# A graph layer with decayed neighbour weights: weight multiplied in at the start, variance by a product with ones, bias with the accumulator's copy, groups closed by transposes, and a new order of all tasks

## The chip, the cores and the metric

The kernel runs on one core of one Trainium2 chip. The metric is device time in microseconds; a timed run is about 2 us longer than the span between the first and the last instruction in its trace. Moments are us from the start of the span.

## The reference, cut to what matters

```python
def _L0_gnn_ref(input, adj, weight, bias):        # MAX_NEIGH 100, DECAY 0.5
    support = input @ weight                      # 4096 x 64 @ 64 x 64
    mask = (adj != 0).astype(support.dtype)       # 4096 x 4096
    rank = jnp.cumsum(mask, axis=1)
    deg = rank[:, -1:]
    k = jnp.minimum(deg, float(MAX_NEIGH))
    pos = rank - (deg - k)
    w = mask * jnp.where(pos > 0, DECAY ** (k - pos), 0.0)
    return w @ support + bias
h = jnp.maximum(_layernorm(x, axis=-1), 0.0)
x = x + _L0_gnn_ref(h, adj, L0_gnn_weight, L0_gnn_bias)
```

The adjacency is 67 MB of float32; x is 1 MB. Everything else is small.

## The kernel before

The adjacency streams in as 64 chunks of 1 MB (128 rows by 2048 columns); four chunks make a unit, two units make a group of 512 output rows. A chunk is converted to bytes by VectorE, some by ScalarE (`signed`), transposed as packed words by TensorE, and settled into SBUF by VectorE. A unit's counts go through `totals` (TensorE), `split` (ScalarE), `suffix` (TensorE) and `clamp` (VectorE). Then, eight times a unit, `place` and `scan` (TensorE) give the exponent, `weigh` (ScalarE) the weight 2^-n, and `aggregate` (TensorE) adds weights times features into one PSUM bank. At a group's end `drain`, `project` (times the weight matrix) and `finish` follow.

The features are prepared once, at the start: turned, centered, squared, reduced, put to the power -1/2 on GpSimd, scaled, and cut in a rounded half and a remainder.

```python
    def center(b0):
        pc = pxs[b0] = ps_v.tile([P, 4, H, D], F32, tag="v", name="pc")
        for b in range(4):
            nc.tensor.matmul(pc[:, b, :, :], xt[:, (b0 + b) * P:(b0 + b + 1) * P], less, start=True, stop=True)
    # ... centered: ScalarE copies pc to xs; square: ScalarE
    def root(h):
        ...
        nc.vector.reduce_sum(var, sqs.pop(h), axis=AX.X)
        nc.vector.tensor_scalar(var, var, EPS, 2.0 ** -76, op0=ALU.add, op1=ALU.mult)
        nc.gpsimd.tensor_tensor(ns[h], var, half.to_broadcast([P, HB]), op=ALU.pow)
    # ... scale, first (rounded copy, ScalarE), second (difference, VectorE)
    def project(g, part=None):
        ...
            nc.tensor.matmul(pts[g][:, tt, :], sums[g][:, tt * P:(tt + 1) * P], w_sb, start=True, stop=True)
```

No engine's instruction order is written by hand. Each task has an engine, a rank, two modelled durations and its needs; a loop in the kernel's own Python picks, engine by engine, the task of lowest rank among those ready within a short wait, and the program is emitted in that order. Each engine then executes its list in order, so a rank or a modelled duration changes the order, and the order is fixed once built.

```python
        task(totals, (u,), PE, 8 * u - 7, 750, 950, ...)
        for k in range(NP):
            task(scan, (u, k), PE, 8 * u + k, 240, 450, [("place", u, k // CB)])
            task(weigh, (u, k), ACT, 8 * u + k, 1000, 1130, [("scan", u, k)], ("w", ("aggregate", u, k)))
            task(aggregate, (u, k), PE, 8 * u + k + 3, 475, 710, ...)
```

## Time and profile before

| | before |
|---|---|
| timed, median of 3 | 210.91 us (210.53 to 211.01) |
| span of the profiled run | 208.8 us |
| TensorE, ScalarE, VectorE busy | 89%, 81%, 71% |
| stream of chunks | 420 GB/s until about 168 us |
| first weigh of unit 0, 1, 15 | 29.0, 46.2, 193.9 us |

Shares of busy time do not decide here, since three engines and the stream run at nearly the same pace. What is read instead is the lag: how long after the landing of a unit's fourth chunk its first weigh starts. The landing is the last of the sixteen that the trace has for each load.

### The profile page before, as it was taken

What the parts mean: (1) busy time and instruction counts of PE and PEld (TensorE: products, weight loads), DVE (VectorE), ACT (ScalarE), POOL (GpSimd) and SP (SyncE); (2) the same over time, 40 slices, a digit from 0 to 9 for tenths busy, and PEclk for the clock granted to TensorE, in tenths of its full rate; (3) what the DMA queues carried; (4) which work ended last, traced back from release to release, by engine and by line L of the source; (5) the groups of instructions that cost most, each with busy time, mean ns of one, the idle gap of its engine ahead of it and who ended that gap; (6) DMA issues with size and microseconds to landing.
All of it is one profiled execution on the core that took longest, in us unless ns stands there. A gap on an engine that the chain in (4) does not pass through costs nothing.

```text
span 208.8 us, 2970 instructions
## 1 busy us (share of the span) xinstructions
PE 186.9 (89%) x1101; PEld 106.9 (51%) x1101; DVE 149.2 (71%) x192; ACT 169.6 (81%) x172; POOL 23.8 (11%) x39
## 2 busy tenths in 40 slices
PE   7299784987999999979999989999999999999972
PEld 2189441544556464645465546556555655554321
DVE  4943999998888797888887896989698974411001
ACT  2066959996997989879999897898989898998870
POOL 6000075050005000200040002000200020001000
PEclk9969999999999999999999999999999999999996
DMA  6999999899999999999999999999999910000000
GB/s 237 424 425 424 419 417 424 342 418 421 425 422 425 419 421 421 424 421 419 422 422 422 421 421 422 424 416 424 417 422 419 383 69 3 0 0 25 0 0 25
DMA packets 10445, 69.45 MB, mean 333 GB/s; under 512 B 1504, under 2 KB 1760, under 8 KB 2240
## 3 DMA queue, kind: packets, MB, share of 16 engines
q1 hardware_dynamic: 9952, 68.29, 78.8%
q0 software_dynamic: 336, 0.92, 1.1%
q8 instruction: 8, 0.13, 0.2%
q10 hardware_dynamic: 144, 0.07, 0.1%
q14 instruction: 5, 0.04, 0.0%
HBM read 68.22 MB, written 1.05 MB: 332 GB/s over the span
## 4 chain that ended last, share of the span: by engine, by line
DMA 52%; PE 30%; DVE 9%; ACT 3%; issue 3%; POOL 1%; DVEq 0%; SPq 0%; ACTq 0%; POOLq 0%
DMA a_sb<-in_adj_dram 52%; PE acc L352 11%; DVE m L288 5%; PE v L339 4%; PE pt L298 4%; ACT wk L344 3%; PE px L233 2%; PE po L375 2%; PE v L336 2%; PE pc L243 2%; PE tot L313 1%; PE ps L324 1%; DVE mt L307 1%; DVE o L381 1%; PE none L225 1%
## 5 line engine op out<-in xcount | busy, mean ns | idle before, releaser
L344 ACT ACTIVATE wk<-v,floor 128x1024 fp32r<-128x1024 uint8 x128 | 134.0, 1120 | 19.3 <-PE v L339 19.1
L352 PE MATMUL acc<-wk,hr 128*128 128x512 f32 x256 | 94.5, 453 | 3.2 <-ACT wk L344 1.7
L288 DVE TENSOR_SCALAR m<-a_sb 128x2048 uint8<-128x2048 f32 x61 | 86.0, 1411 | 15.5 <-DMA a_sb<-in_adj_dram 15.4
L352 PEld LDWEIGHTS acc<-wk,hr 128*128 128x128 f32 x256 | 40.8, 189 | 22.6 <-issue 10.2
L298 PE MATMUL pt<-ident,m 128*128 128x128 f32 x256 | 44.9, 275 | 7.4 <-DVE m L288 4.0
L307 DVE COPY mt<-pt 128x512 uint32<-128x512 uint32 x61 | 41.1, 686 | 12.0 <-PE pt L298 11.9
L339 PE MATMUL v<-mt,tri 128*128 128x512 f16 x128 | 45.9, 395 | 0.0
L298 PEld LDWEIGHTS pt<-ident,m 128*128 128x128 f32 x256 | 32.9, 140 | 23.5 <-issue 6.0
L339 PEld LDWEIGHTS <-tri 128*128 128x128 f16 x128 | 10.4, 98 | 20.4 <-issue 19.3
L383 POOL DMA_DIRECT2D out_dram<-o x7 | 5.1, 733 | 132.0 <-DVE o L381 112.8
L318 ACT ACTIVATE sums<-tot 128x1024 f16<-128x1024 uint8 x16 | 16.5, 1033 | 0.9 <-PE tot L313 0.8
L330 DVE TENSOR_SCALAR behind<-ps,excess 128x512 f16<-128x512 f32 x16 | 11.9, 744 | 5.1 <-PE ps L324 4.1
L336 PE MATMUL v<-behind,where 32*128 32x512 f16 x128 | 14.0, 384 | 0.9 <-DVE behind L330 0.8
L313 PE MATMUL tot<-mt,band 128*32 128x512 f16 x128 | 10.2, 393 | 3.4 <-DVE mt L307 2.9
L237 ACT ACTIVATE xt<-px 64x512 f32<-64x512 f32 x8 | 4.4, 588 | 10.4 <-PE px L233 10.4
L225 PE MATMUL none<-junk 128*128 128x512 bf16 x36 | 10.4, 424 | 1.3 <-DVE junk L128 1.3
L324 PE MATMUL ps<-sums,later 128*128 128x512 f16 x32 | 9.6, 380 | 1.0 <-ACT sums L318 0.8
L367 DVE COPY acc_sb<-acc 128x256 f32<-128x256 f32 x1 | 0.4, 425 | 13.7 <-PE acc L352 13.7
L375 PEld LDWEIGHTS po<-w_sb,acc_sb 128*128 128x128 f32 x64 | 8.1, 191 | 3.5 <-ACT acc_sb L369 1.4
L375 PE MATMUL po<-w_sb,acc_sb 128*128 128x64 f32 x64 | 8.4, 274 | 1.4 <-ACT acc_sb L369 1.0
L267 POOL TENSOR_TENSOR rstd<-var,half 128x16 f32<-128x16 f32 x2 | 6.8, 3396 | 24.7 <-DVE var L266 24.7
L357 POOL TENSOR_TENSOR xr<-xr,bias_sb 128x256 f32<-128x256 f32 x8 | 8.4, 1053 | 7.3 <-DMA bias_sb<-in_L_gnn_bias_dram 7.1
(68 smaller groups left out, 76.5 us busy)
## 6 DMA issues: line engine op xcount, KB each, us to landing
a_sb<-in_adj_dram SPq DMA_DIRECT2D x64, 1024.0 KB, 18.4
xr<-in_x_dram SPq DMA_DIRECT2D x2, 512.0 KB, 7.8
out_dram<-o POOLq DMA_DIRECT2D x7, 128.0 KB, 5.6
out_dram<-o ACTq DMA_DIRECT2D x1, 64.0 KB, 1.8
out_dram<-o SPq DMA_DIRECT2D x1, 64.0 KB, 1.8
w_sb<-in_L_gnn_weight_dram SPq DMA_DIRECT2D x2, 16.0 KB, 16.4
bias_sb<-in_L_gnn_bias_dram SPq DMA_DIRECT2D x1, 32.0 KB, 13.8
```

What stands on the lines that cost most here:

```text
L225: nc.tensor.matmul(none, junk[:, :P], junk, start=True, stop=True)
L288: nc.vector.tensor_scalar(m_v, a_v, 0.0, 64.0, op0=ALU.not_equal, op1=ALU.add)
L298: nc.tensor.transpose(pts[u, tt][:, c, :], m32[:, c * P:(c + 1) * P], ident)
L307: nc.vector.tensor_copy(mw, pt)
L313: nc.tensor.matmul(tot[SUB * c:SUB * (c + 1), :], band[:, SUB - 4 - 4 * a:2 * SUB - 4 - 4 * a], masks[u][:, c, :, a], start=(a == 0), stop ...
L318: nc.scalar.activation(sums8[u], pts.pop((u, "n")).bitcast(U8).rearrange("p (i f) -> p f i", f=4)[:, 1:3, :], AF.Copy)
L330: nc.vector.tensor_scalar(behind[u], pts.pop((u, "s")), excess, float(MAX_NEIGH), op0=ALU.subtract, op1=ALU.min)
L336: nc.tensor.matmul(v, where[q, a, :], behind[u][q, :], start=True, stop=False)
L339: nc.tensor.matmul(vs[u, k], tri, masks[u][:, k % CB, :, k // CB], start=False, stop=True)
L344: nc.scalar.activation(wts[u, k], v, AF.Exp, scale=-LN2, bias=floor)
L352: nc.tensor.matmul(accs[0], hr[:, h * HB + k // CB * 2 * CB + s * CB + k % CB, :, :].rearrange("p s d -> p (s d)"), wk[:, s, :], start=((h ...
L375: nc.tensor.matmul(pts[g][:, tt, :], sums[g][:, tt * P:(tt + 1) * P], w_sb, start=True, stop=True)
```

## The change

Its intent: take work off the start and off the end of each group. The arithmetic:

```diff
+    def center(n):                      # 512 columns at once, transposed layout kept
+        nc.tensor.matmul(pxs[n], less.rearrange("p h d -> p (h d)"), xt[:, n * W:(n + 1) * W], start=True, stop=True)
+    def square(n): ...  def relu(n): ... # ScalarE, both from PSUM
+    def spread(n):                      # variance by a product with ones
+            nc.tensor.matmul(pxs["var"][:, b, :], sq[:, b, :], ones, start=True, stop=True)
+    def support(n):                     # the weight multiplied in at once
+            nc.tensor.matmul(pp[:, b, :, :], rx[:, 4 * n + b, :], w2.rearrange("p h d -> p (h d)"), start=True, stop=True)
-        nc.vector.reduce_sum(var, sqs.pop(h), axis=AX.X)
...
-            nc.scalar.activation(sums[g][:, r], accs[0][:, r], AF.Copy)
-            nc.tensor.matmul(pts[g][:, tt, :], sums[g][:, tt * P:(tt + 1) * P], w_sb, start=True, stop=True)
-        nc.vector.tensor_add(outs[g][:, r, :], pts[g][:, r, :], xbs[g][:, r, :])
+            nc.scalar.activation(sums[g][:, r], accs[0][:, r], AF.Identity, bias=bias_sb)
+            nc.tensor.transpose(pts[g][:, tt, :, :].rearrange("p s d -> p (s d)"), sums[g][:, tt * P:(tt + 1) * P], ident)
+        nc.vector.tensor_add(outs[g][:, r, :], pts[g][:, r, 0, :], xr[...][:, r, :])
+        nc.vector.tensor_add(outs[g][:, r, :], pts[g][:, r, 1, :], outs[g][:, r, :])
```

and the schedule (cut):

```diff
-signed = (4, 8, 11)                                   # chunks converted by ScalarE
+signed = (4, 5)
-        task(fetch, (r,), SP, 2, 0, 0, [])            # x after two chunks
+        task(fetch, (r,), SP, 0.5, 0, 0, [])          # after one
-            task(settle, (u, tt), DVE, 8 * u - 12 + 2 * tt, ...
+            task(settle, (u, tt), DVE, 8 * u - 18 + 2 * tt, ...
-        task(totals, (u,), PE, 8 * u - 7, ...
+        task(totals, (u,), PE, 8 * u - 3, ...
-            task(scan, (u, k), PE, 8 * u + k, ...
+            task(scan, (u, k), PE, 8 * u + k + 0.5, ...
-            task(aggregate, (u, k), PE, 8 * u + k + 3, ...
+            task(aggregate, (u, k), PE, 8 * u + k + 14, ...
-    wait = 60, 250, 60, 60, 0
+    wait = 60, 150, 600, 60, 0
-            lag = max(landed - at, 2100) + (2470 if f is load else 1240)   # modelled landings
+            lag = max(landed - at, 2450) + (2480 if f is load else 1280)
```

## The prediction

> **What bounds the kernel now.** The work is cut into 16 units of four adjacency chunks. A unit's chunks are loaded, converted to bytes, transposed, settled into SBUF and counted (totals, split, suffix, clamp); then, eight times, TensorE scans, ScalarE weighs (an exponential) and TensorE aggregates. I read the slices of the page first, to see which stage has which limit.
>
> ```profile
> PE   7299784987999999979999989999999999999972
> ACT  2066959996997989879999897898989898998870
> PEclk9969999999999999999999999999999999999996
> DMA  6999999899999999999999999999999910000000
> GB/s 237 424 425 424 419 417 424 342 418 421 425 422 425 419 421 421 424 421 419 422 422 422 421 421 422 424 416 424 417 422 419 383 69 3 0 0 25 0 0 25
> ```
>
> The DMA rows stand at 420 GB/s from the second slice to the thirty-first and then stop: 64 chunks stream at line rate, and no change of compute makes that shorter. But the kernel goes on for some 42 us after the stream, with TensorE and ScalarE full. So the question is how far compute lags behind the stream. Second view: the busy times by stage, cut at the points where the lag can be read (columns: window, its length, busy us and instructions of PE, weight load, VectorE, ScalarE, GpSimd, then granted clock, DMA share, GB/s).
>
> ```profile
> 10.70:29.00 18.30, 16.33 (x117) 12.63 (x116) 11.76 (x16) 11.95 (x17) 2.86 (x1) 0.91 1.01 422
> 29.00:46.20 17.20, 13.43 (x81) 6.70 (x79) 16.63 (x19) 16.84 (x15) 6.68 (x4) 1.00 0.96 397
> 46.20:102.00 55.80, 52.62 (x311) 30.17 (x309) 46.36 (x49) 48.05 (x49) 3.94 (x4) 1.00 1.01 422
> 102.00:169.50 67.50, 66.00 (x409) 38.05 (x407) 57.94 (x64) 60.59 (x62) 5.30 (x7) 1.00 0.98 406
> 169.50:193.90 24.40, 23.81 (x138) 13.00 (x137) 7.97 (x12) 22.24 (x24) 1.52 (x3) 1.00 0.03 11
> 193.90:208.80 14.90, 9.25 (x37) 4.01 (x35) 0.91 (x3) 8.62 (x9) 0.00 (x0) 0.88 0.03 9
> ```
>
> ScalarE first weighs at 29.0; the second unit's weighs start at 46.2; the last unit's at 193.9, and from there the end is 14.9 us away, whatever came before. The reader is to see the third row, 29 to 46.2: ScalarE is busy 16.84 of 17.20 us but finishes one unit in it, where a later unit takes 10.5. What fills it is in the ScalarE timeline (start, length, instruction; in brackets the idle before it):
>
> ```profile
> 24.43 1.01 ACT L318 ACTIVATE sums<-tot 128x1024 f16<-128x1024 uint8 x1
> 28.99 1.11 ACT L344 ACTIVATE wk<-v,floor 128x1024 fp32r<-128x1024 uint8 x1 [2.61 <-PE v L339]
> 30.00 2.48 ACT L286 ACTIVATE m<-a_sb 128x2048 int8<-128x2048 f32 x1
> 32.34 1.03 ACT L274 ACTIVATE hr<-xs 128x1024 fp32r<-128x1024 f32 x1
> ...
> 37.49 1.06 ACT L274 ACTIVATE hr<-xs 128x1024 fp32r<-128x1024 f32 x1
> 38.46 2.53 ACT L286 ACTIVATE m<-a_sb 128x2048 int8<-128x2048 f32 x1
> 40.84 4.11 ACT L344 ACTIVATE wk<-v,floor 128x1024 fp32r<-128x1024 uint8 x4
> ```
>
> In those 17.2 us eight weighs and one split for the next unit take about 9.2; two converts of 2.5 us and two rounding copies of the features (L274) of 1 us take 7. To get the lag I set the landing of each unit's fourth chunk (last of the sixteen landings of its DMA) against the unit's first weigh: unit 0 15.4 and 29.0 (lag 13.6), unit 1 26.8 and 46.2 (19.4), unit 7 88.4 and 110.4 (22.0), unit 15 169.5 and 193.9 (24.4). Most of the lag is made in the start phase, another 5 us creep in over fourteen units. The start-up of the features is thus not a small prelude but the lag that every later unit carries, because nothing later is fast enough to catch up:
>
> ```profile
> L344 ACT ACTIVATE wk<-v,floor 128x1024 fp32r<-128x1024 uint8 x128 | 134.0, 1120 | 19.3 <-PE v L339 19.1
> L352 PE MATMUL acc<-wk,hr 128*128 128x512 f32 x256 | 94.5, 453 | 3.2 <-ACT wk L344 1.7
> L339 PE MATMUL v<-mt,tri 128*128 128x512 f16 x128 | 45.9, 395 | 0.0
> L375 PE MATMUL po<-w_sb,acc_sb 128*128 128x64 f32 x64 | 8.4, 274 | 1.4 <-ACT acc_sb L369 1.0
> ```
>
> Per unit: DMA 4 x 2.48 us between landings, about 10.1 with the output writes. ScalarE 8 weighs at a pitch of 1.03 (the four of 4.13 us below, less overlap) = 8.2, a split 0.95, half a drain 0.27: 9.5. TensorE, from the chain of waits, which is unbroken TensorE from 150 to 182 us: starts of a unit's placement at 151.79, 161.63, 172.20 and 181.82, so 10.0 per unit with one projection in three; with one in two 10.15. Three rates within 6% of each other; the observed cadence is (193.9 - 46.2)/14 = 10.55.
>
> ```profile
> 184.16 0.59 ACT L369 ACTIVATE acc_sb<-acc 128x512 f32<-128x512 f32 x1
> 193.88 4.13 ACT L344 ACTIVATE wk<-v,floor 128x1024 fp32r<-128x1024 uint8 x4 [0.42 <-PE v L339]
> ```
>
> **What the Trainium skill says.** ScalarE: Activation LUTs, section "What ACT_TABLE_LOAD costs": an activation with immediates takes 186 ns plus 0.833 ns per element, a per-partition pointer for the bias adds about 93 ns, and back-to-back ones overlap by 93. The trace agrees: 613 for 512 elements against 590 measured for the drain (line 184.16 above), 1133 for the weigh with its pointer against 1120. So the bias put into the drain costs an estimated 0.09 us each, off seven drains 0.6 us. TensorE: Matmul & The Clock Gate, section "What's actually happening": the array falls to half clock after an idle window of about 3.4 us and needs as long to recover. Here TensorE idles 4.03 us before its first transpose at 9.59, and the clock is 0.91 in 10.7 to 29: 18.3 x 0.09 = 1.65 us lost just while it turns the features. VectorE: DVE Perf Modes, "Why PSUM operands drop a tier": an fp32 PSUM source runs at one element per cycle; the clamp, 128x512 from PSUM, takes 744 ns, so I size the new scale by that. DMA: Bandwidth & Descriptors, "Why small descriptors are slow (HBM only)", bears on weight and bias, 64 KB in rows of 256 B: below 512 B a fixed overhead for each descriptor counts. Slice 8 dips to 342 GB/s where they land, 5.2 x (1 - 342/420) = 1.0 us of stream.
>
> **The change, part by part.** (a) Features first: after one chunk rather than two. They landed at 9.2 and 10.4; one chunk less is 2.5 us earlier, 6.7 and 7.9. That also meets the warm-up matmuls that end at 5.6, so the half-clock stretch should mostly vanish: 2.5 + up to 1.6 = about 4 us on the feature path.
> (b) The feature path. Before: turns until 16.0, centers to 20.9, then four copies and a square on ScalarE (to 24.5), a reduce of 1.22, a power of 3.9 on GpSimd (to 30.0), scale 1.23, rounding copy at 32.3, difference until 36.2; first aggregate 36.4. After: turns from 7 to 12.3 (eight ScalarE copies of 0.59 bind), four centers, eight square/relu activations of 0.59 until about 17.5, the sums of squares by 32 short TensorE instructions of 0.1 (no reduce: -2 x 1.21 us VectorE), powers in two halves of 2.9 to 3.9 ending at about 19.5 and 23, weight product 32 x 0.117 = 3.7 us beside the first power, scale 4 x 0.74, halves rounded and subtracted. First half of the features ready at about 23, all by 26: some 10 us earlier than 36.2. TensorE pays 3.3 + 3.7 us more, of which 23 warm-up matmuls after 10 us (5 us of filler) show that there is room.
> (c) Converts on ScalarE: chunks 4 and 5 instead of 4, 8 and 11. They land at 17.9 and 20.4, when ScalarE has finished the features and has no scan yet: it converts until about 23, then splits, and the first weigh comes at 23 + 1.0 split + 0.7 suffix + 0.7 clamp + 0.9 place and scan = about 26.5 (29.0 before). From there no convert interrupts: 8.2 weighs + 0.95 split + four rounding halves 2.4 = 11.5, so unit 1 weighs from about 38, not 46.2. Lag there 12 instead of 19.4. Gain on the path: 8 us. This is the main term.
> (d) End of a chunk group: 8 projection instructions (0.84 us in the chain) become 4 transposes at 0.11 = 0.44. Saves 0.4 per pair of units, 0.2 per unit of TensorE: 10.15 becomes 9.95, under the DMA's 10.1. The finish doubles on VectorE (0.42 to about 0.85 per pair), which has idle time from DMA waits there. At the very end 1.1 of projection becomes about 0.5 and one add of 0.29 becomes two: -0.3.
> (e) Weight and bias transfers: 1 us of the stream's dip gone, fourth chunk of the last unit at about 168.3 instead of 169.5.
> (f) Ranks: aggregates are put 14 ranks behind their unit, scans and settles ahead, so that ScalarE's food comes first and aggregates fill. ScalarE waits for scans 16.0 us between 46 and 194; a part of this should go, but five PSUM buffers for groups of four still force a gap (0.42 before the group at 193.88 shown above, when nothing else competes). I take cadence 10.2 instead of 10.55.
> Sum: unit 1's weighs at 38, fourteen units of 10.2 make 180.8; the DMA bound with lag 12 says 180.3. I allow 2 us for mismatches of the fixed order: 182.7. Plus 14.6 for the last unit is a span of 197.3; the timed median is 2.1 above the span (210.91 against 208.8): 199.4. I predict 199.5.
>
> **Rivals.** R1, TensorE takes over the start: from 7 to 38 us it must do the turns (4-5), centers (2-3.5; whether 512 fp32 columns go in 0.44 or 0.85 us no row shows), sums 3.3, weight product 3.7, two units without aggregates (2 x 6.2), transposes of a third, first aggregates 3.7: 31 of 31 us. If short instructions or waits cost more, unit 1 starts at 41 to 42 and the lag stays 16: about 203. R2, the cadence does not improve: the units stay at 10.55 because the group-of-four gap and not the order causes it; then 38 + 14 x 10.55 + 14.6 + 2.1 = 202.4. R3, both, with a clock drop from a badly guessed start: 206, "same". R4, the order fits so well that lag stays at 11 and the stream alone binds: 168.3 + 11 + 14.6 + 2.1 = 196. Against a loss: no part adds to the steady-state engines more than 0.1 us per drain and 0.4 of VectorE per pair, and the stream leaves 42 us to win from.
>
> **Range and chances.** R4 and R2/R1 span 195.5 to 205, which I give 8 in 10. Within 2% means above 206.7; that needs R3. Faster 0.91, same 0.07, slower 0.02.
>
> **What would show it.** Right: first aggregate near 24 to 28; no ScalarE convert after 25 us; unit 1's weighs at 36 to 40; stream's end near 168; last unit's first weigh 10 to 13 us earlier than 193.9, TensorE less than full in mid-kernel with waits on chunks; turn-back at 0.44 per group. Wrong: a first weigh later than 29, clock below 0.9 in the first 30 us, ScalarE waits for scans still near 16 us, or a lag that grows by more than 4 us between units 1 and 15.

## The result, and the profile after

The changed kernel takes 197.78 us (197.62 to 197.88, 4 runs) against 210.72 us (4 runs) beside it: ratio 0.9384, 95% interval 0.9368 to 0.9400. Ratios here are the mean time of one kernel's fast runs over that of the other's in the same rounds, so not quite the ratio of the medians. The prediction was 199.5 in a range of 195.5 to 205.

The slices of the changed kernel's page, PE and DMA rows (tenths of busy time, each slice 4.9 us):

```profile
PE   7699988999999996999999999999999999998981
DMA  6999999999999999999999999999999999100000
```

The stream still fills thirty-three slices; what has shrunk is the part behind it. The stages, cut at the corresponding points (columns as in the prediction's second view):

```profile
10.70:29.70 19.00, 17.80 (x126) 13.01 (x125) 13.67 (x19) 13.65 (x19) 6.20 (x2) 1.00 1.01 421
29.70:39.70 10.00, 9.42 (x56) 4.99 (x55) 10.00 (x13) 9.14 (x10) 0.00 (x0) 1.00 1.01 419
39.70:102.00 62.30, 59.79 (x368) 36.64 (x369) 55.70 (x65) 57.61 (x59) 4.53 (x3) 1.00 1.01 420
102.00:168.00 66.00, 63.68 (x392) 37.82 (x390) 57.27 (x66) 62.33 (x64) 4.00 (x3) 1.00 1.00 413
168.00:180.10 12.10, 11.82 (x66) 6.56 (x64) 3.44 (x5) 11.43 (x12) 0.00 (x0) 1.00 0.00 1
180.10:195.90 15.80, 10.56 (x50) 7.34 (x50) 2.41 (x7) 8.83 (x10) 0.54 (x1) 0.98 0.05 17
```

Unit 0's weighs take 10.0 us (row 29.70 to 39.70), not 17.2. ScalarE is busy 9.14 of 10 there, and nothing but weighs and one split is in it. Its timeline:

```profile
18.55 4.88 ACT L306 ACTIVATE m<-a_sb 128x2048 int8<-128x2048 f32 x2
25.35 1.02 ACT L338 ACTIVATE sums<-tot 128x1024 f16<-128x1024 uint8 x1 [1.92 <-PE tot L333]
...
29.67 3.13 ACT L364 ACTIVATE wk<-v,floor 128x1024 fp32r<-128x1024 uint8 x3 [0.44 <-PE v L359]
32.78 1.02 ACT L338 ACTIVATE sums<-tot 128x1024 f16<-128x1024 uint8 x1
33.70 5.13 ACT L364 ACTIVATE wk<-v,floor 128x1024 fp32r<-128x1024 uint8 x5
39.69 3.13 ACT L364 ACTIVATE wk<-v,floor 128x1024 fp32r<-128x1024 uint8 x3 [0.86 <-PE v L359]
```

The two converts, at 18.55, now lie before any weigh, and the five weighs at 33.70 are followed at 39.69 by unit 1's. Where the whole 12.9 us of span came from:

| stretch | before | after | difference |
|---|---|---|---|
| start to unit 1's first weigh | 46.2 | 39.7 | -6.5 |
| fourteen units, to unit 15's first weigh | 147.7 (10.55 each) | 140.4 (10.03 each) | -7.3 |
| from there to the end | 14.9 | 15.8 | +0.9 |
| span | 208.8 | 195.9 | -12.9 |

The table says when the time was won, not by which edit; the experiments below show that a late start can be made up in part.

The lag was 19.4 us at unit 1 and grew to 24.4 at unit 15; it is now 12.7 at unit 1, 12.6 at unit 8 and 12.1 at unit 15. The units keep step with the stream, whose last chunk lands at 168.0 (169.5 before).

The first weigh, however, is no earlier: 29.7 against 29.0. The chain of waits through the start (start, length, what) says why:

```profile
12.67 3.44 PE pc L250 x8
16.11 3.48 PE pd L262 x32
19.61 0.27 DVE var L267 x2
...
19.94 6.21 POOL rstd L271 x2
...
26.18 1.29 DVE xs L280 x2
...
28.11 0.74 DVE behind L350
```

TensorE centers for 3.44 us, then sums squares for 3.48, and only when all sums are there do the two powers run, one behind the other, 6.21 us; the scale of the second half starts at 26.18. Unit 0's transposes queue on TensorE meanwhile and its counts end in the split at 25.35, for which ScalarE has waited 1.92 us. The suffix behind that split ends on TensorE at 27.0, but its clamp (the last line) stands in VectorE's list behind the scale and a settle and starts at 28.11.

At a group's end, by form (count, busy us, mean ns), 32 closing transposes stand for the 64 projection instructions of before, and the drain with its bias takes 712 ns instead of 590:

```profile
L391 PE MATMUL po<-ident,acc_sb 128*128 128x128 f32 x32 | 5.0, 278 | 1.9 <-ACT acc_sb L385 1.7 <-DVE behind L350 0.2
L385 ACT ACTIVATE acc_sb<-acc,bias_sb 128x512 f32<-128x512 f32 x7 | 5.0, 712 | 0.4 <-PE acc L372 0.4
```

### The profile page after: what moved, and what is told of

Same layout as the page of the kernel before. It is cut to its first block, busy times and chain, and to the rows that moved or that the text cites. A ratio compares the mean times of both kernels' runs of the same rounds, so it can differ in the third digit from the quotient of the medians.

```text
span 195.9 us, 2956 instructions
## 1 busy us (share of the span) xinstructions
PE 180.9 (92%) x1091; PEld 111.3 (57%) x1093; DVE 149.4 (76%) x210; ACT 167.0 (85%) x175; POOL 18.7 (10%) x30
## 4 chain that ended last, share of the span: by engine, by line
DMA 61%; PE 22%; DVE 9%; POOL 3%; ACT 2%; issue 1%; SPq 1%; DVEq 0%; ACTq 0%
DMA a_sb<-in_adj_dram 61%; PE acc L372 9%; DVE m L308 6%; POOL rstd L271 3%; PE v L359 3%; PE pt L318 2%; PE pd L262 2%; PE pc L250 2%; ACT wk L364 1%; PE v L356 1%; PE po L391 1%; PE tot L333 1%; PE ps L344 1%; DVE xs L280 1%; DVE mt L327 1%
## 5 line engine op out<-in xcount | busy, mean ns | idle before, releaser
L364 ACT ACTIVATE wk<-v,floor 128x1024 fp32r<-128x1024 uint8 x128 | 133.4, 1133 | 10.3 <-PE v L359 10.2
L372 PE MATMUL acc<-wk,hr 128*128 128x512 f32 x256 | 80.4, 432 | 0.4 <-DVE hr L290 0.4
L372 PEld LDWEIGHTS acc<-wk,hr 128*128 128x128 f32 x256 | 44.9, 188 | 18.7 <-issue 7.4
L318 PEld LDWEIGHTS pt<-ident,m 128*128 128x128 f32 x256 | 30.4, 141 | 24.5 <-issue 4.7
L359 PE MATMUL v<-mt,tri 128*128 128x512 f16 x128 | 42.3, 389 | 0.0
L400 POOL DMA_DIRECT2D out_dram<-o x7 | 9.1, 1296 | 147.6 <-DVE o L398 147.6
L359 PEld LDWEIGHTS <-tri 128*128 128x128 f16 x128 | 12.2, 97 | 7.0 <-issue 4.1
L356 PE MATMUL v<-behind,where 32*128 32x512 f16 x128 | 12.6, 384 | 0.0
L333 PE MATMUL tot<-mt,band 128*32 128x512 f16 x128 | 10.1, 392 | 0.0
L356 PEld LDWEIGHTS <-where 32*128 32x128 f16 x128 | 3.3, 91 | 10.7 <-issue 10.7
L397 DVE TENSOR_TENSOR o<-po,xr 128x256 f32<-128x256 f32 (+1 forms) x9 | 3.5, 384 | 5.6 <-PE po L391 5.6
L271 POOL TENSOR_TENSOR rstd<-var,half 128x16 f32<-128x16 f32 x2 | 6.2, 3109 | 15.3 <-DVE var L267 15.3
L233 PE MATMUL none<-junk 128*128 128x512 bf16 x18 | 6.0, 474 | 1.4 <-DVE junk L126 1.2
L385 ACT ACTIVATE acc_sb<-acc,bias_sb 128x512 f32<-128x512 f32 (+1 forms) x8 | 5.5, 682 | 2.1 <-DVE acc_sb L383 1.7
```

Source lines behind the costliest of these rows:

```text
L271: nc.gpsimd.tensor_tensor(ns[i].rearrange("p b h -> p (b h)"), var.rearrange("p b h -> p (b h)"), half.to_broadcast([P, HB]), op=ALU.pow)
L318: nc.tensor.transpose(pts[u, tt][:, c, :], m32[:, c * P:(c + 1) * P], ident)
L333: nc.tensor.matmul(tot[SUB * c:SUB * (c + 1), :], band[:, SUB - 4 - 4 * a:2 * SUB - 4 - 4 * a], masks[u][:, c, :, a], start=(a == 0), stop ...
L356: nc.tensor.matmul(v, where[q, a, :], behind[u][q, :], start=True, stop=False)
L359: nc.tensor.matmul(vs[u, k], tri, masks[u][:, k % CB, :, k // CB], start=False, stop=True)
L364: nc.scalar.activation(wts[u, k], v, AF.Exp, scale=-LN2, bias=floor)
```

## The experiments

Twelve kernels ran, nine made from the changed kernel and three from the kernel before. They ran in three sessions on two chips, each beside the kernel before, whose medians there were 210.65, 210.71 and 210.45 us; so times are set against each other across sessions to some 0.3 us. All gave correct results except the two half-stream kernels, which are wrong on purpose. The theory to be tested is that of the prediction: the start sets a lag that is carried, the new order lowers the pace from 10.55 to the stream's, and the shorter group end helps TensorE a little. Its rivals: the arithmetic alone does it, or the order alone does it. The table gives each result, with the moments read from its profiled run (us; a unit's pace is the distance from unit 1's to unit 15's first weigh over 14).

| run | time | ratio to before | unit 1 | unit 15 | a unit | to the end |
|---|---|---|---|---|---|---|
| before | 210.7 | 1 | 46.2 | 193.9 | 10.55 | 14.9 |
| after | 197.78 | 0.938 | 39.7 | 180.1 | 10.03 | 15.8 |
| former ranks | 204.09 | 0.969 | 40.2 | 187.2 | 10.50 | 15.2 |
| transposes twice | 199.05 | 0.945 | 42.7 | 180.9 | 9.87 | 16.6 |
| three chunks on ScalarE | 203.52 | 0.966 | 45.3 | 186.8 | 10.11 | 15.1 |
| features after two chunks, list made anew | 204.46 | 0.971 | 45.7 | 186.2 | 10.04 | 15.2 |
| features after two chunks, order kept | 199.72 | 0.950 | 44.4 | 182.3 | 9.85 | 15.8 |
| model's pitch 2.47 | 200.07 | 0.950 | 40.9 | 183.0 | 10.15 | 15.3 |
| weight late | 202.15 | 0.960 | 44.2 | 185.5 | 10.09 | 15.0 |
| half the stream | 190.94 | 0.907 | 38.4 | 173.1 | 9.62 | 15.8 |
| before, new ranks | 208.99 | 0.993 | 45.9 | 191.6 | 10.41 | 15.3 |
| before, whole new schedule | 208.32 | 0.990 | 40.9 | 191.4 | 10.75 | 15.1 |
| before, half the stream | 206.92 | 0.981 | 47.8 | 190.4 | 10.19 | 14.9 |
| tail | 197.04 | 0.936 | 40.8 | 180.0 | 9.94 | 15.6 |

### The former ranks in the changed kernel

```diff
-  convert 8u-17, settle 8u-18, totals 8u-3, split 8u-2.5, suffix 8u-3.5, place 8u+k-0.5, scan 8u+k+0.5, weigh 8u+k+2.5, aggregate 8u+k+14, closing 8u+13; wait 60, 150, 600, 60, 0
+  convert 8u-15, settle 8u-12, totals 8u-7, split 8u-7,   suffix 8u-6,   place 8u+k-1,   scan 8u+k,     weigh 8u+k,     aggregate 8u+k+3,  closing 8u+12; wait 60, 250, 60, 60, 0
```

> The changed kernel with the former ranks and waits of the list for the steady state (convert, settle, totals, split, suffix, place, scan, weigh, aggregate), all other parts of the change kept. If the order gives the cadence, as I now think (10.55 to 10.03 us a unit, fourteen units): the cadence goes back to 10.3 or more and the time to 202 or more. If the removed projection and the shorter start give the whole gain and the order nothing: 198, within 1 us of the changed kernel. If the order is everything: 207 or more.

204.09 us, all runs within 0.5. Unit 1 starts as in the changed kernel (40.2), but a unit takes 10.50 again, almost what it took before the change. So between these two lists the ranks are worth 6.3 us, all of it pace; how much of that another list with the same ranks would move is asked below. The stage from 102 to 165 us, first the changed kernel and then this one:

```profile
102.00:165.00 63.00, 60.68 (x374) 36.02 (x373) 54.30 (x62) 59.33 (x61) 2.85 (x2) 1.00 1.01 421
```

```profile
102.00:165.00 63.00, 58.77 (x360) 33.16 (x359) 53.29 (x61) 56.11 (x57) 2.78 (x3) 1.00 1.01 420
```

In the same 63 us TensorE executes 374 instructions in one and 360 in the other, and ScalarE 61 against 57, at the same stream. With the former ranks both engines stand idle more often: between 46 and 180 us ScalarE waits 11.3 us for scans instead of 8.1.

### Half the stream

Each chunk's first half alone is loaded and converted twice. Order, instruction counts and everything else are the base kernel's; in the stage from 102 to 165 us the mean lengths of convert, settle, scan and aggregate agree with the base kernel's within 1%, so lighter traffic did not make the instructions themselves faster.

```diff
-        nc.sync.dma_start(tiles[n], adj_v[:, ..., h * (N // H):(h + 1) * (N // H)])
+        nc.sync.dma_start(tiles[n][:, :N // H // 2], adj_v[:, ..., h * (N // H):h * (N // H) + N // H // 2])
-        m_v, a_v = m8.rearrange("p q e -> p e q"), tiles.pop(n).rearrange("p (e q) -> p e q", e=E)
+        m_v = m8.rearrange("p q (a e) -> p a e q", a=2)
+        a_v = tiles.pop(n)[:, :N // H // 2].rearrange("p (e q) -> p e q", e=2).unsqueeze(1).to_broadcast([P, 2, 2, Q])
```

On the changed kernel:

> The changed kernel with only the first half of each chunk loaded (and used twice, so the result is wrong on purpose): the stream needs 1.25 us a chunk, all else is in the same order. If the stream sets the cadence: it falls from 10.03 to what TensorE and ScalarE allow, 9.5 to 9.9, and the time by 2 to 7 us, to 191 to 196. If TensorE or ScalarE set it: within 1 us of 197.8.

190.94 us; the pace falls from 10.03 to 9.62. The same stage:

```profile
102.00:165.00 63.00, 62.79 (x386) 39.09 (x384) 56.31 (x65) 61.39 (x63) 3.99 (x3) 1.00 0.50 160
```

With the stream at half, TensorE is busy 62.79 of 63 us and ScalarE 61.39. So at full width the stream sets the pace of the changed kernel, and TensorE is right behind it, 4% faster. On the kernel before:

> The kernel before with half of each chunk loaded, likewise. If its 10.55 a unit comes from TensorE and the fixed order, with the stream well ahead (lag 19 to 24 us): within 1.5 us of 210.8. If the stream had a part in it: 207 or less.

206.92 us, ratio 0.981 (0.978 to 0.984), a gain clear of noise though not clearly of 2%: I had expected 209 or more, because the stream was 19 to 24 us ahead of the weighs. The pace falls from 10.55 to 10.19, so the stream had a part in it although it was far ahead. This is the same stage, before at the full stream and then at half:

```profile
102.00:165.00 63.00, 61.50 (x377) 35.42 (x375) 53.71 (x60) 56.44 (x58) 4.96 (x6) 1.00 1.01 421
```

```profile
102.00:165.00 63.00, 62.88 (x400) 37.22 (x397) 54.47 (x60) 58.38 (x60) 4.49 (x6) 1.00 0.54 173
```

TensorE goes from 61.50 to 62.88 busy us with 377 and 400 instructions. The converts stand in VectorE's fixed list between the settles of an older unit. My reading is that when a convert waits for its chunk, the older unit's settle behind it waits too, and TensorE with it; half a stream takes that wait away. The waits fit this: between 46 and 180 us VectorE waits 13.7 us for chunks before and not at all at half the stream, and the waits of TensorE and its weight loads for VectorE's results fall from 8.8 us in sum to 1.2. The gain is measured and these waits go with it; no run takes away the order alone. The two kernels also give the paces that compute alone allows in these two orders: 10.19 a unit before, which is slower than the stream's 10.03, and 9.62 after, which is faster.

### The new ranks, and the whole new schedule, in the kernel before

The reverse of the first experiment: the new ranks and waits in the kernel before, and then also the features after one chunk and chunks 4 and 5 on ScalarE. Both keep the former modelled landings and engine start times, so the second is the whole new schedule but for these numbers.

```diff
-    wait = 60, 250, 60, 60, 0          # and the ranks as above, former to new
+    wait = 60, 150, 600, 60, 0
     # second kernel, in addition:
-    signed = (4, 8, 11);  task(fetch, (r,), SP, 2, ...);    task(load, (n,), SP, n if n < 2 else n + 2, ...)
+    signed = (4, 5);      task(fetch, (r,), SP, 0.5, ...);  task(load, (n,), SP, n, ...)
```

> The kernel before with the new ranks and waits of the steady state alone; features, loads, converts on ScalarE and projection as before. If the order gives the cadence: a cadence of 10.1 to 10.25 (TensorE's 10.15 is now the floor) in place of 10.55, so 205 to 207. If the order does nothing without the shorter start and the lighter end: 210 to 211. A slower result would say that the new ranks only fit the new parts.

> The kernel before with all of the new schedule (ranks, waits, features after one chunk, chunks 4 and 5 on ScalarE) and none of the new arithmetic. If the schedule is the cause and the arithmetic small: 200 to 203. If the new arithmetic of the features (no wait for a reduce, halves) and the end is needed: 205 or more.

208.99 and 208.32 us: neither is faster by 2%. The first has a pace of 10.41, not the 10.1 to 10.25 that I expected of the order alone. The second wins the start (unit 1 at 40.9, 5.3 us earlier) and loses 2.8 us of it on the way, at 10.75 a unit. So the order is not the cause by itself: the same ranks with the old arithmetic give a poor order, and the former ranks with the new arithmetic do too. In the second kernel's trace ScalarE waits 16.1 us for scans between 46 and 180 us (8.1 in the changed kernel), and TensorE's transposes wait for splits. Why this list came out worse than that of the kernel with the weight late (below), which differs in the feature path, in when weight and bias are loaded and in those modelled landings and start times, I could not settle; one altered modelled number alone moved another kernel by 2.3 us (below).

### Closing transposes twice

```diff
+            for _ in range(2):
                 nc.tensor.transpose(pts[g][:, tt, :, :].rearrange("p s d -> p (s d)"), sums[g][:, tt * P:(tt + 1) * P], ident)
```

> The changed kernel with every closing transpose done twice, so that TensorE spends per group of units about what the projection took (8 short instructions, some 0.85 us, in place of 4). If the cadence was won by TensorE work taken away (9.95 against 10.15 a unit): up to 0.2 x 14 = 2.8 us more, 200 to 200.6. If the stream sets the cadence and TensorE has room: less than 0.6 us more, most of it at the last unit (4 more transposes, 0.4 us).

199.05 us, 1.3 more. Unit 15 starts only 0.8 us later, and the last stage is 0.8 longer (16.6). In the profiled run TensorE's clock was 0.89 over the first 30 us and unit 1 came 3.0 us late; by unit 15 most of that was made up, at 9.87 a unit. So as much TensorE work as the projection held costs 1.3 us, between my two expectations, and TensorE has room.

### A later start, three ways

Chunks 4, 8 and 11 on ScalarE as before the change; the features fetched after two chunks; and the same late features with the order of every other engine kept. In the third only the transfers' issue order is swapped when the program is emitted; a comparison of the two programs showed the lists of TensorE, VectorE and ScalarE to be identical to the changed kernel's.

```diff
-signed = (4, 5)
+signed = (4, 8, 11)
```
```diff
-        task(fetch, (r,), SP, 0.5, 0, 0, [])
+        task(fetch, (r,), SP, 1.5, 0, 0, [])
```
```diff
     for at, _, f, args in sorted(order, key=lambda o: o[:2]):
+        if f is fetch and args == (0,):
+            load(1)
+        if f is load and args == (1,):
+            continue
```

> The changed kernel with chunks 4, 8 and 11 converted by ScalarE, as before, in place of 4 and 5. If what is lost at the start is carried to the end, as the prediction's sum has it: one more convert of 2.5 us and two of them between the weighs of units 0 and 1 make unit 1 weigh 2.5 to 5 us later and the time 200 to 203. If later units catch up, because the cadence possible is below the stream's 10.03: unit 1 later by the same, but the lag back at 12 to 13 us by unit 8 and the time within 1 us of 197.8.

> The changed kernel with the features fetched after two chunks, as before, not after one: they land 2.5 us later. Carried to the end: unit 1 weighs 2 us or more later and the time is 199.5 to 201. Caught up, or hidden because unit 0 waits for its fourth chunk and for VectorE rather than for the features: within 1 us of 197.8.

> The changed kernel with the features again fetched after two chunks (2.5 us later), but with every other engine's instructions in exactly the changed kernel's order. If a late start is carried to the end by itself: unit 1 weighs 2.5 us later (3 to 5 if the clock drops too) and the time is 200 to 203, like the 204.5 of the run with the list made anew. If the list's order made that loss, and with a good order later units catch up (half the stream showed 9.61 us a unit possible, 10.03 is the stream): unit 1 later, the lag back at 12 to 13 us by unit 10, and the time within 1 us of 197.8.

The first takes 203.52 us. One convert now lies just before the first weigh, which starts at 32.1, and one between the weighs of unit 0, as these lines of its ScalarE timeline show:

```profile
29.71 2.58 ACT L306 ACTIVATE m<-a_sb 128x2048 int8<-128x2048 f32 x1
37.05 2.52 ACT L306 ACTIVATE m<-a_sb 128x2048 int8<-128x2048 f32 x1
```

Unit 1 comes 5.6 us later and the end 5.7: all of it is carried. The second takes 204.46 (203.15 to 206.13; the profiled run is the fastest), with unit 1 at 45.7 and likewise all of it carried. Both lose more than I had expected. The third takes 199.72: unit 1 comes 4.7 us late (the late features and a clock of 0.89 in the first 30 us), the pace is 9.85, and unit 15 is 2.2 us late: the lag is 18.8 at unit 1, 16.4 at unit 10, where I had expected 12 to 13, and 14.2 at unit 15. So a late start by itself is more than half made up. The rest of the second kernel's loss, 4.7 us by the medians and 3.4 between the two profiled runs, which had the same clock of 0.89 in the first 30 us, comes from the list that was made anew. In that list the later units keep the stream's pace at a lag of about 17 to 20 us and do not use the room that the third kernel uses. The first kernel's list is new too, so how much of its 5.7 us is the converts' own stays open.

### A number in the model that costs nothing

```diff
-            lag = max(landed - at, 2450) + (2480 if f is load else 1280)
+            lag = max(landed - at, 2450) + (2470 if f is load else 1280)
```

> The changed kernel with one number of the list's model altered that costs nothing by itself: it reckons with 2.47 us a chunk, not 2.48. The same instructions come in another order. If the ranks make good orders in general: within 1.5 us of 197.8. If the order of this kernel is a lucky one among many that the ranks give: 200 or more, and then the 4 to 6 us of the runs with a new list cannot be put down to their own cause.

200.07 us (199.92 to 200.20), 2.3 more than the changed kernel, for one altered modelled number: same instructions, other order. An order made anew thus moves the time by a couple of us without any cause of its own. Differences of that size between kernels with different lists cannot be put down to the edit. The 5.7 us of the three chunks and the 6.3 us of the ranks are 2.5 to 3 times as large, but this is one sample, and the two kernels with late features are another, 3.4 to 4.7 us apart by their lists alone. By my own expectation above, the sizes of the runs with a new list are therefore not their edits' alone. This kernel has the new ranks as well and still takes 4.0 us less than that with the former ranks, so the direction of that experiment holds in both lists and its size is 4.0 to 6.3 us.

### The weight late in the changed kernel

The early product is with an identity; the group ends as before, with projection, bias added to x on GpSimd, and one add.

```diff
-        nc.scalar.dma_start(w2[h * D:(h + 1) * D, h, :], weight)
+        nc.scalar.dma_start(w_sb[h * D:(h + 1) * D, :], weight)
+        nc.vector.tensor_copy(w2[q, h, :], ident[q, q])
-            nc.tensor.transpose(pts[g][:, tt, ...], sums[g][:, tt * P:(tt + 1) * P], ident)
+            nc.tensor.matmul(pts[g][:, tt, :], sums[g][:, tt * P:(tt + 1) * P], w_sb, start=True, stop=True)
```

> The changed kernel with the weight multiplied in at the end, as before: the early product is one with an identity (same cost), and each group ends with projection, bias added to x on GpSimd and one add. If the end of a group (0.2 us of TensorE a unit) is what the kernel before with the new schedule lacks: cadence 10.4 or more and 203 to 208. If the shorter feature path is: cadence 10.0 to 10.2 and 198 to 200.5.

202.15 us: between the two expectations. The pace is 10.09, which speaks for the feature path; but the start is late too: the second half of x lands at 9.9 us instead of 8.3, presumably behind the bias, which is now broadcast in rows of 256 B at that time, and the clock was 0.89 over the first 30 us. Against the kernel with an equally late start and the order kept (unit 1 at 44.4 and 44.2), it is 2.4 us slower. Not all of this is the old group end: the fourth chunk of unit 15 lands at 169.6, there at 168.1, and another list alone may bring as much. So the cost of the old group end is not shown to differ from zero.

### The tail

```diff
-            task(split, (u,), ACT, ...)                 # and drain of group 6, and the halves of the last drain
+            task(split, (u,), DVE if u == U - 1 else ACT, ...)
-                task(drain, (g,), ACT, ...
+                task(drain, (g,), DVE if u == U - 3 else ACT, ...
-                    task(drain, (g, part), DVE if part else ACT, ...
+                    task(drain, (g, part), ACT if part else DVE, ...
```

> The changed kernel, order the same up to about 170 us; then ScalarE, which is full from the stream's end to its last weigh, gives the last split (1.03 us) and the last full drain (0.68) to VectorE, idle there, and the final drain's first half goes to VectorE, which drains first, so that its transposes need not wait for ScalarE's half. If ScalarE's work bounds the tail: 1.2 to 2.3 us less, 195.5 to 196.6. If TensorE's order or the last unit's latency bounds it: within 0.6 us of 197.8.

197.04 us (196.95 to 197.29). The ratio to before, 0.936 (0.934 to 0.938), and that of the changed kernel, 0.938 (0.937 to 0.940), overlap, so the 0.7 us between the medians, taken in two sessions, is not a clear gain. The last weighs on ScalarE:

```profile
175.87 8.35 ACT L364 ACTIVATE wk<-v,floor 128x1024 fp32r<-128x1024 uint8 x8 [0.71 <-PE v L359]
185.06 4.13 ACT L364 ACTIVATE wk<-v,floor 128x1024 fp32r<-128x1024 uint8 x4 [0.85 <-PE v L359]
```

The split and the drain are gone from the list, but ScalarE then waits for scans, 0.71 and 0.85 us, and its last weigh ends at 189.2 us in both kernels. So ScalarE's work did not bound the tail. The chain that ended last has TensorE in its place: it runs without a break from 180.35 to 190.26 us in the changed kernel and from 180.11 to 190.24 in this one. The last four scans are placed at 183.76 (183.74 here), after ten aggregate instructions, and twenty more, which the new rank puts late, close the stretch (changed kernel):

```profile
185.67 4.59 PE acc L372 x20
```

The five PSUM buffers for scans also allow the last four placements only after the third of the four weighs before. I ran nothing that takes either away.

## Why the prediction was right

Total and sign were right: 197.8 in a range of 195.5 to 205, at a predicted 199.5. Term by term the sum was less good than its total, whose closeness is in part luck, since the misses cancel: unit 1 at 38 was 39.7 (+1.7), fourteen units of 10.2 and 2 us for mismatches, 144.8, were 140.4 (-4.4), and the last stage 14.6 was 15.8 (+1.2).

(a) Features earlier: said to land at 6.7 and 7.9, landed at 7.2 and 8.3, and the half-clock stretch is gone in the profiled run (clock 1.00 from 10.7 on). Right for that run; the other three had mean clocks of 0.983, 0.998 and 0.989 over the span against 0.999, so such stretches come back in some executions; those runs took at most 0.26 us more.

(b) The feature path: said 10 us earlier, first half ready at 23. The first aggregate started at 31.5 against 36.4. The step that failed is the power in two halves at 19.5 and 23: both waited for the last sum at 19.6 and ended at 26.15. The first aggregate then also waited for its difference, which stood on VectorE behind the clamp, a convert and a settle until 30.6. The centers also took the larger of my two values, 0.86 each, since 512 fp32 columns cost two instructions of 0.43.

(c) Converts on ScalarE: said done by 23 and the first weigh at 26.5. The converts ended at 23.4, but the split waited for TensorE until 25.35, the clamp for VectorE until 28.11, and the first weigh came at 29.7. This is the rival R1 in a mild form: TensorE full at the start, 17.80 of 19.0 us. The last us is VectorE's order, which no rival had. The second half of the step held better than I put it: 10.0 us of weighs instead of 11.5, because the rounding copies fitted in before. The run with three chunks puts unit 1 back by 5.6 us, in a list of its own.

(d) Group end: said 0.2 us a unit of TensorE, 2.8 in all. Doubling the transposes cost 1.3; restoring the old end cost 2.4 with another list and a later stream, so that run does not size it. The transposes start 0.11 us apart, as said. Right in kind, at or below the size said. The closing stage, said to shrink by 0.3, grew by 0.9: unit 15's weighs take 9.1 us against 8.7, and from the last weigh to the end it is 6.7 us against 6.2, where drains with bias (0.50 and 0.48 against 0.44 and 0.39) and two adds a half instead of one stand in a row: the adds take 1.14 us instead of 0.49, more than the 0.45 that the transposes save.

(e) Stream's end: said 168.3, measured 168.0. Right.

(f) Order: said 10.2 a unit instead of 10.55, got 10.03. The runs show this term to be larger than (d) in the steady state: 4.0 to 6.3 us in the new arithmetic, by two lists with the new ranks, and only 1.7 us in the old. What I had not seen is that most of the ranks' gain comes only with the new arithmetic; with the former ranks the rest of the change still saves 6.6 us.

Two statements of the prediction fell. "Nothing later is fast enough to catch up" fits the kernel before, whose lag only grows, and the lists made with a late start; in the changed kernel's own order, 4.7 us of delay became 1.9 at the end. And R4, the stream alone binding at 196, which I had as the optimistic edge, is nearly what happened: lag 12 to 13, not 11. R2, the pace unchanged, is out. Of the prediction's own signs one of those for wrong came true, a first weigh later than 29 (29.7), and two of those for right were missed: the first aggregate at 24 to 28 (31.5), and unit 15 earlier by 10 to 13 us (13.8). ScalarE's waits for scans fell from 14.4 to 8.1 us between 46 and 180.

Two slips of the prediction change little: the row "29 to 46.2" that it calls the third is the second of those shown, and unit 1 at 38 with its fourth chunk at 26.8 is a lag of 11.2, not 12.

What stays open: which of the ranks carries the 4.0 to 6.3 us, why the kernel before with the whole new schedule runs at 10.75, what the converts and the group end are worth apart from their lists, and what the tail would take if the aggregates came earlier.

## What to carry to other kernels

When every engine is within a few per cent of the transfers, read the lag behind the stream at several units instead of shares of busy time: a lag made at the start, one that grows and one in the tail have different cures. With a fixed order per engine, an engine that waits for a chunk also holds what stands behind it, so that a stream far ahead may still slow the kernel; here half the stream made the kernel before 1.9% faster. When a list scheduler orders the program, test an edit with the order kept as well, and alter a harmless number once to see how much the order alone moves the time: here 2.3 us, and 3.4 to 4.7 in the pair with late features.

## What the Trainium skill lacked or had wrong

- TensorE: Matmul & The Clock Gate, "Back-to-back issue gap", gives a sustained 131 ns per matmul of 512 columns. In the kernel before two aggregates of 512 columns (fp32r) take 0.46 to 0.47 us in an unbroken chain, 0.23 each, and two f16 products of the suffix 0.43, near the 216 ns that the page gives for an isolated one.
- ScalarE: Activation LUTs, "What ACT_TABLE_LOAD costs", says that a pointer for the bias adds about 93 ns; the drain went from 590 to 712, 122 ns.
- No page that I found sizes a power on GpSimd: 128x16 elements took 2.9 to 3.9 us, 3.1 and 3.4 on average in the two kernels, which made it the longest single step of the start.
- No page has how much a fixed order alone moves a kernel with all engines near their limit: 2.3 us for an altered model number, 3.4 to 4.7 for a list made anew with late features.
